# An attention kernel's context and output products moved later by one slot, and a key copy moved ahead of the divisions

## The chip, the cores and the metric

The kernel runs on one NeuronCore of a Trainium2 chip. The metric is the device time of one execution in microseconds, as the median of several runs. The engines are named as in the profile: PE is TensorE's matmul, PEld its weight load, DVE is VectorE, ACT is ScalarE, POOL is GpSimd and SP the engine that issues the DMAs.

## The reference

The input is x, 4 x 1024 tokens of 512 features, all in fp32. The result is x plus an attention of the layer-normalized x plus a matmul of it in rounded 8-bit floats. Cut to what matters here:

```python
xn = layernorm(x)
q  = rope(rmsnorm(xn @ Wq + bq))            # 16 heads of 128
lk = rope(rmsnorm(xn @ Wlk + blk)); lv = xn @ Wlv + blv
entries = weighted sums of each 4 tokens of xn        # 256 for each batch
ck = rope(rmsnorm(entries @ Wk + bk)); cv = entries @ Wv + bv
sparse = softmax(top 8 of causal(q @ ck.T)) @ cv
local  = softmax(band(q @ lk.T)) @ lv                 # this and the previous 128 tokens
out    = x + ((sparse + local) * 0.5) @ Wo + bo + fp8(xn) @ fp8(input2)
```

## The kernel before

The tokens are cut into 32 tiles of 128 (8 for each batch of 1024; the tile's number in its batch is called c). The 16 heads make 8 units of two heads. So there are 256 pairs of a tile and a unit, numbered n = 8t + u, and the main loop runs over slots s, each of which works on several of them at different stages. The order of the instructions on every engine is the order of the program (a manual schedule); each engine works its own list in that order, and only data and buffers hold it up.

The steps of a unit n, with the slot in which each stands before the change:

- `queries(n)` in slot n-3: q and local keys of two heads in one PSUM bank `qp`, eight matmul rows of 512 columns (L591).
- `squares`, `spread` (slot n-3, ACT and POOL) and `normalize`, `go_on_rotating`, `end_rotation` (slot n-2, DVE and POOL): the norms and the rotation.
- `turn_keys` and `fetch_keys` (slot n-2): DVE transposes blocks, SP stores them to DRAM and fetches them turned, as `qT` and `lkT`. In the first tile TensorE turns them instead.
- `values_of(n)` in slot n-1: the value projection, eight matmul rows of 256 columns (L697); `keep_values` copies it to `lv`.
- `scores(n, h)` at the head of slot n: for each head, against the previous tile's keys, this tile's keys and the entries' keys `ckT` (L739, L746, L749), into two PSUM banks `sc`. There is one such buffer.
- `weigh`, `settle`, `divide` in slot n: mask, top 8, exponentials (L799, L807), sums, and the division of the probabilities on ACT (L832).
- `turn(n)` in slot n: DVE transposes the probabilities in blocks of 32 to `probB` (L850), and SP stores them to DRAM (L858, `pr`). `fetch(n)` at the end of slot n: SP fetches them turned as `probT` in four DMAs (L892). `probT` has one buffer.
- `values(n)` in slot n+1: the context, up to 16 matmul rows of 128 columns (L909), with `probT` as the moving operand.
- `keep_context(n)` in slot n+2: ACT copies the context to `cT` (L924).
- `to_output(n)` in slot n+2: the product with Wo (L942), four matmul rows of 512 columns, accumulated over the eight units of a tile in one PSUM bank `out`, of which there is one. Behind unit 7, DVE adds the bank to the tile `x_sum` (L951), and SP stores the tile.

In a steady slot TensorE's order is scores(s), queries(s+3), to_output(s-2), values_of(s+1), values(s-1). `by_dma(n)` is true for the units from 8 to 252, whose probabilities are turned by DMA; for the others TensorE turns them (`turn_here`, `keep_turned`).

Beside this, generators are advanced at fixed places of a slot by `steps()` and `until(...)`. `chunk_prep` normalizes a later tile and pools its tokens to entries; in tiles 1 to 3 it runs for two tiles at once. `chunk_entries` makes the keys and values of new entries: it begins at u = 4 of a tile in `made` (0 to 4, then every fourth from 7 to 27), and its last step, at u = 7, turns the keys on TensorE (L557) and copies them to `ckT` on ACT (L558). `chunk_eight` makes the 8-bit product of a tile (L573). All of them and `values_of` share two PSUM banks `pp`.

The last three units stand behind the loop, written out by hand.

Of the kernel before, what the change touches and what calls it, by code (L numbers as in the profile page):

```python
# [38 lines left out]
def kernel(  # L39
# [30 lines left out]
    NCH = S // P  # L70
    NU = NH // 2
# [421 lines left out]
    def chunk_entries(g, n):  # L493

        b, half = divmod(g, NCH // GC)
        if b not in entries:
            entries[b] = (
                work.tile([P, 2 * P], F32, tag="ckT", name=f"ckT_{b}"),
                [None, None],
            )  # L500
        ckT, cv = entries[b]
        if n == 1:
            few = few_here[0]
        else:
            few = work.tile([P, HID], F32, tag="kv", name=f"fewT_{g}_{n}", bufs=1)
            if n < GC:
                nc.gpsimd.memset(few, 0.0)
            if not g:
                nc.sync.dma_start(few[:, 0 : NE * KK], few_here[1])
            turned = pooled[g].rearrange("c (a i) (b x) -> b i (c a) x", a=NB, b=NB)  # L510
            lo = 0 if g else 1
            for i in range(NB):
                nc.sync.dma_start(
                    few[ds(i * BLK, BLK), lo * P : n * P].rearrange("i (a x) -> i a x", x=BLK),
                    turned[i][:, lo * NB : n * NB],
                )
        few = few.rearrange("p (n k) -> p n k", k=KK)
        cse = cse_here if n == 1 else load_entry_angles(half)
        yield "A4"
        ep = pp(f"ep_{g}_{n}")  # L520
        for k in range(KK):
            nc.tensor.matmul(  # L522
                ep[:, 0 : 2 * D],
                few[:, :, k],
                wkv_sb[:, k, :],
                start=(k == 0),
                stop=(k == KK - 1),
            )
        yield "A5"
        kv = work.tile([P, HID], F32, tag="kv", name=f"kv_{g}_{n}", bufs=1)  # L530
        spare = kv[:, 2 * D :]
        kv = kv[:, 0 : 2 * D].rearrange("p (h d) -> p h d", h=2)
        nc.vector.tensor_tensor(
            kv.rearrange("p h d -> p (h d)"), ep[:, 0 : 2 * D], bkv_sb, ALU.add
        )

        cv[half] = work.tile([P, D], F32, tag=f"cv_{half}", name=f"cv_{g}_{n}")
        nc.scalar.copy(cv[half], kv[:, 1, :])
        ess = work.tile([P, 1], F32, tag="ess", name=f"ess_{g}_{n}", bufs=1)
        square_sum(ess, kv[:, 0, :], f"e{g}_{n}")  # L540
        er = rstd_of(ess, 1, 1.0 / D, EPS_RMS, f"er_{g}_{n}")
        yield "B5"
        ck = kv[:, 0:1, :]
        nc.vector.scalar_tensor_tensor(
            ck[:, 0, :], ck[:, 0, :], er, norm_w[:, 1, :], ALU.mult, ALU.mult
        )
        rotation = rotate(
            ck, cse, 1, spare[:, 0:ROPE], f"e{g}_{n}", spare[:, ROPE : 2 * ROPE]
        )
        next(rotation)  # L550
        next(rotation)
        yield "A6"
        for _ in rotation:
            pass
        yield "B6"
        cp = pp(f"cp_{g}_{n}")
        nc.tensor.transpose(cp[:, 0:P], ck[:, 0, :], ident)  # L557
        nc.scalar.copy(ckT[:, ts(half, P)], cp[:, 0:P])  # L558
        yield "A7"

# [79 lines left out]
    def by_dma(n):  # L640

        return NU <= n < NN - 3
# [292 lines left out]
    def to_output(n):  # L935
        t, u = place(n)
        b, c = divmod(t, NCH)
        if u == 0:
            outs[t] = psum.tile([P, HID], F32, tag="out", name=f"op_{t}", bufs=1)
        op, cT = outs[t], units[n].pop("cT")  # L940
        for h in range(2):
            nc.tensor.matmul(  # L942
                op,
                cT[:, h, :],
                wo_sb[u][:, h, :],
                start=(u == 0 and h == 0),
                stop=(u == NU - 1 and h == 1),
            )
        if u == NU - 1:
            xt = x_tiles.pop(("sum", t))  # L950
            nc.vector.tensor_tensor(xt, xt, op, ALU.add)  # L951
            nc.sync.dma_start(out[b, ts(c, P), :], xt)
# [15 lines left out]
    def for_unit(n, *todo):  # L968
        if 0 <= n < NN:
            for f, *more in todo:  # L970
                f(n, *more)
# [29 lines left out]
    for s in range(-3, NN - 3):  # L1001
        t, u = place(s)

        if u == 6 and t + 1 in ready:
            regular = chunk_prep(ready[t + 1][0])
        if u == 3 and 0 <= t < NT:
            load_x(t, "sum")
        if u == 4 and t in made:
            begun = chunk_entries(*made[t])
            next(begun)  # L1010
        if u == 5 and t in made:
            running.append(begun)
        if u == 5 and 0 <= t < NT:
            running.append(chunk_eight(t))
        if u == 4 and 0 <= t and t + 1 in ready:
            load_x(ready[t + 1][0], "norm")

        for_unit(s, (scores, 0), (scores, 1))
        for_unit(s - 2, (keep_context,))
        if s < NU - 1:  # L1020
            for_unit(s + 1, (turn_keys_here,), (keep_keys,))
        for_unit(s, (weigh,))
        for_unit(s + 3, (queries,))
        if s < 0:
            if s == -3:
                for _ in first:
                    pass
            if s == -1:
                until(start, "A7")
        for_unit(s + 2, (normalize,))  # L1030
        for_unit(s, (settle,))
        for_unit(s, (divide,))

        if 0 <= s < NU:
            fold_first_row(s)
        for_unit(s + 2, (go_on_rotating,), (end_rotation,))
        if by_dma(s):
            turn(s)
        if s + 2 >= NU:
            for_unit(s + 2, (turn_keys,))  # L1040
        steps()
        host = t if u < 4 else t + 1
        if host in ready:
            until(regular, FIRST_HALF.get(u))
        two = len(ready.get(t, ())) == 2
        if two and u == 2:
            extra = chunk_prep(ready[t][1])
        if two:
            until(extra, FIRST_HALF_MORE.get(u))
        for_unit(s + 3, (squares, (0, 1, 2, 3)), (spread,))  # L1050
        for_unit(s - 2, (to_output,))
        steps()
        if host in ready:
            until(regular, SECOND_HALF.get(u))
        if two:
            until(extra, SECOND_HALF_MORE.get(u))
        for_unit(s + 1, (values_of,))
        if not by_dma(s):
            for_unit(s, (turn_here,))
        for_unit(s - 1, (values,))  # L1060
        if by_dma(s):
            fetch(s)
        else:
            for_unit(s, (keep_turned,))
        if s + 2 >= NU:
            for_unit(s + 2, (fetch_keys,))
        for to, what in stores:
            nc.sync.dma_start(to, what)
        stores.clear()
        if u == 2 and 0 <= t < NT - 1:  # L1070
            fetch_tokens(t + 1)
        if u == 3 and 0 <= t < NT - 1:
            fetch_with_ones(t + 1)
        if two and u == 1:
            load_x(ready[t][1], "norm", True)
        for_unit(s + 1, (keep_values,))
        if s == -2:
            until(start, "B5")
        if s < NU:

            if s == -2:
                late_loads()
            if s == -1:
                late_constants()
                for k in range(KK):
                    nc.sync.dma_start(w2_raw[k], input2[ts(k, P), :])
            if 0 <= s < KK:
                for _ in range(4):
                    next(rounding, None)
            if 3 <= s + 6 < NU:  # L1090
                load_wqk(s + 6, nc.sync)
            if 3 <= s + 4 < NU:
                load_wlv(s + 4, nc.sync)
            if 0 <= s + 1 < NU:
                load_wo(s + 1, nc.sync)
        if u == 6 and 0 <= t and t + 2 < NT:
            load_angles(t + 2)
        units.pop(s - 1 - NU, None)


    a, b, c = range(NN - 3, NN)
    eight = chunk_eight(NT - 1)
    next(eight)
    for_unit(a, (scores, 0), (scores, 1))
    keep_context(a - 2)
    weigh(a)
    normalize(c)
    settle(a)
    divide(a)
    go_on_rotating(c)  # L1110
    end_rotation(c)
    turn_keys(c)
    to_output(a - 2)
    for n in (b, c):
        values_of(n)
        keep_values(n)
    fetch_keys(c)
    for_unit(b, (scores, 0), (scores, 1))
    next(eight)
# [20 lines left out]
    for _ in eight:  # L1140
        pass
    to_output(b)
    for_unit(c, (turn_here,), (keep_turned,), (values,), (keep_context,), (to_output,))


# [44 lines left out]
```

## Time and profile before

| what | us |
|---|---|
| median of 3 runs | 2650.33 (2649.67 to 2651.03) |
| the profiled execution's own time | 2650.34 |
| its span, from the first to the last instruction | 2648.6 |
| PE busy | 2608.5 (98%) |
| PEld busy | 1785.3 (67%) |
| DVE busy | 2215.5 (84%) |
| ACT busy | 1391.1 (53%) |
| POOL busy | 781.6 (30%) |

The granted TensorE clock is 0.999 of full speed over the span. The ends of matmuls are modelled and the matmuls overlap, so durations of a PE row are not to be added; the starts are. A row of a group has the busy time, the mean of one instruction in ns, and the engine's idle time before it with what ended it. A row of the waits has the total, the number and the longest.

### The profile page before, as it was taken

The numbers are of one execution on the slowest core, as the hardware profiler recorded it, in microseconds if no ns is written. First come the engines' busy times: TensorE is split into PE (matmuls) and PEld (weight loads), VectorE is DVE, ScalarE is ACT, GpSimd is POOL, SyncE is SP. The second block draws the span as 40 slices with busy tenths as digits, with TensorE's granted clock in tenths as the row PEclk, the third lists the DMA queues.
The fourth block names the chain that finished last, engine by engine and source line by source line (L and its number), as shares of the span: only waits on it lengthen the run. The fifth ranks groups of instructions, "written<-read, shape, count | busy, mean of one in ns | idle before, by whom it ended". The sixth has DMA issues, their size and how long they took to land.

```text
span 2648.6 us, 46831 instructions
## 1 busy us (share of the span) xinstructions
PE 2608.5 (98%) x11852; PEld 1785.3 (67%) x11887; DVE 2215.5 (84%) x8381; ACT 1391.1 (53%) x5560; POOL 781.6 (30%) x1128
## 2 busy tenths in 40 slices
PE   7999999999999999999999999999999999999998
PEld 4666667677666666766766666667676666676776
DVE  6878888888888888888988888888888888877886
ACT  3545545555555555555555555555555555554555
POOL 3422333223332223232233222232323332322222
PEclk9999999999999999999999999999999999999999
DMA  7355556665655555666655556665665555566554
GB/s 252 100 151 159 146 143 177 177 167 160 165 143 158 158 149 162 165 175 174 163 154 145 157 150 159 170 167 160 173 178 146 149 148 150 150 168 172 158 151 112
DMA packets 721004, 421.15 MB, mean 159 GB/s; under 512 B 395599, under 2 KB 670304, under 8 KB 720736
## 3 DMA queue, kind: packets, MB, share of 16 engines
q1 hardware_dynamic: 720128, 417.75, 58.2%
q8 instruction: 97, 1.59, 0.3%
q14 instruction: 171, 1.40, 0.2%
q10 hardware_dynamic: 608, 0.41, 0.1%
HBM read 224.75 MB, written 193.20 MB: 158 GB/s over the span
## 4 chain that ended last, share of the span: by engine, by line
PE 84%; DVE 7%; ACT 3%; DMA 2%; SPq 1%; issue 1%; POOL 1%; ACTq 0%; DVEq 0%; POOLq 0%
PE qp L591 28%; PE op L942 14%; PE vp L697 14%; PE cp L909 13%; PE sc L749 5%; PE sc L746 4%; PE sc L739 4%; ACT prob L832 1%; ACT prob L799 1%; PE fp L573 1%; DVE sc L771 1%; DVE taken L797 1%; DVE probB L850 1%; SPq L680 1%; PE ep L522 1%
## 5 line engine op out<-in xcount | busy, mean ns | idle before, releaser
L591 PE MATMUL qp<-wqk,xnT 128*128 128x512 f32 x1552 | 709.4, 593 | 4.8 <-DMA wqk<-in_L_attn_Wlk_dram 4.8
L799 ACT ACTIVATE prob<-sc,neg 128x256 f32<-128x256 f32 (+1 forms) x512 | 236.1, 461 | 773.6 <-DVE taken L797 752.4
L591 PEld LDWEIGHTS qp<-wqk,xnT 128*128 128x128 f32 x1552 | 294.9, 190 | 373.3 <-issue 370.9
L832 ACT ACTIVATE prob<-prob,tot 128x256 f32<-128x256 f32 (+7 forms) x1024 | 381.9, 443 | 296.7 <-DVE tot L825 296.7
L697 PEld LDWEIGHTS vp<-wlv,xnT 128*128 128x128 f32 x2048 | 389.0, 190 | 161.6 <-issue 115.3
L697 PE MATMUL vp<-wlv,xnT 128*128 128x256 f32 x2048 | 483.7, 379 | 0.1
L942 PE MATMUL op<-wo,cT 128*128 128x512 f32 x1024 | 481.6, 593 | 1.6 <-ACT cT L924 1.5
L323 POOL TENSOR_TENSOR rb<-th,cs 128x256 f32<-128x256 f32 x256 | 204.0, 797 | 743.8 <-DVE th L619 740.0
L771 DVE CUSTOM_DVE_ANT_0 sc<-sc,mask_b 128x256 f32<-128x256 f32 (+1 forms) x512 | 211.9, 414 | 182.6 <-PE sc L749 172.1
L942 PEld LDWEIGHTS op<-wo,cT 128*128 128x128 f32 x1024 | 193.6, 190 | 227.3 <-issue 185.3
L850 DVE STREAM_TRANSPOSE probB<-prob 128x512 f32<-128x512 f32 (+2 forms) x490 | 306.0, 629 | 10.9 <-ACT prob L832 0.2
L301 POOL TENSOR_SCALAR r<-ss 128x4 f32<-128x4 f32 x256 | 57.7, 226 | 846.8 <-ACT junk L307 844.1
L909 PE MATMUL cp<-probT,lv 128*128 128x128 f32 x1920 | 298.6, 275 | 5.8 <-DMA probT<-pr 4.4
L307 ACT ACTIVATE junk<-qp 128x128 bf16<-128x128 f32 x1024 | 278.6, 272 | 30.0 <-PE qp L599 5.6
L909 PEld LDWEIGHTS cp<-probT,lv 128*128 128x128 f32 x1920 | 273.3, 191 | 23.2 <-issue 10.1
L619 DVE SCALAR_TENSOR_TENSOR th<-qp,r,norm_w 128x128 f32<-128x128 f32 x1024 | 286.2, 342 | 1.9 <-POOL r L302 1.5
L302 POOL TENSOR_TENSOR r<-r,nhalf 128x4 f32<-128x4 f32 x256 | 265.1, 1035 | 21.4
L815 DVE SCALAR_TENSOR_TENSOR prob<-taken,prob 128x128 f32<-128x128 bf16 (+7 forms) x512 | 186.4, 365 | 97.6 <-ACT prob L807 96.4
L591 PE MATMUL qp<-wqk,xone 128*128 128x512 f32 x496 | 258.3, 602 | 1.6 <-DMA xone<-xb_dram 1.4
L909 PE MATMUL cp<-probT,cv 128*128 128x128 f32 x1536 | 255.2, 275 | 0.0
L749 PE MATMUL sc<-ckT,qT 128*128 128x96 f32 (+7 forms) x1024 | 226.7, 303 | 7.0 <-ACT ckT L558 7.0
L909 PEld LDWEIGHTS cp<-probT,cv 128*128 128x128 f32 x1536 | 212.7, 192 | 0.0
(141 smaller groups left out, 3670.5 us busy)
## 6 DMA issues: line engine op xcount, KB each, us to landing
pr<-probB SPq DMA_DIRECT2D x125, 512.0 KB
probT<-pr SPq DMA_DIRECT2D x500, 128.0 KB
qk<-thb SPq DMA_DIRECT2D x992, 64.0 KB
pr<-probB SPq DMA_DIRECT2D x96, 384.0 KB
probT<-pr SPq DMA_DIRECT2D x384, 96.0 KB
qT<-qk SPq DMA_DIRECT2D x248, 128.0 KB
lkT<-qk SPq DMA_DIRECT2D x248, 128.0 KB
x_norm<-_attn_hidden_states_dram SPq DMA_DIRECT2D x32, 256.0 KB
```

Of the source, the lines that this page charges most:

```text
L302: nc.gpsimd.tensor_tensor(r, r, nhalf[: ss.shape[0], 0:n], ALU.pow)
L307: nc.scalar.activation(junk[: src.shape[0]], src, AF.Square, accum_out=acc)
L591: nc.tensor.matmul(qp, xnT[:, k, :] if k or not t else xone, wqk_sb[u][:, k, :], start=(k == 0), stop=(t > 0 and k == KK - 1),)
L619: nc.vector.scalar_tensor_tensor(th[:, i, :], qp[:, ts(i, D)], r[:, i : i + 1], norm_w[:, i // 2, :], ALU.mult, ALU.mult,)
L697: nc.tensor.matmul(vp[:, 0:256], xnT[:, k, :], wlv_sb[u][:, k, :], start=(k == 0), stop=(k == KK - 1),)
L749: nc.tensor.matmul(sc[:, spa], q, ckT[:, 0:m], start=True, stop=True)
L771: nc.vector.tensor_tensor_reduce(sc[h][:, loc], sc[h][:, loc], mask_b[:, loc], -1.0, TAKEN, ALU.add, ALU.min, neg[h][0],)
L799: nc.scalar.activation(probs[h][:, loc], sc[h][:, loc], AF.Exp, bias=neg[h][0], scale=-1.0, accum_out=tot[:, h, 0:1],)
L832: nc.scalar.mul(probs[h][:, cols], probs[h][:, cols], tot[:, h, part : part + 1])
L850: nc.vector.transpose(pb[:, :, ds(h * g, g), :], prob[:, parts[0] * P : (parts[-1] + 1) * P].rearrange("p (g b i) -> p b g i", b=NB, i=BLK),)
L909: nc.tensor.matmul(blocks(cp[:, h, :]), v, probT[:, :, h * len(parts) + i - parts[0], :], start=(i == parts[0]), stop=(i == parts[-1]),)
L942: nc.tensor.matmul(op, cT[:, h, :], wo_sb[u][:, h, :], start=(u == 0 and h == 0), stop=(u == NU - 1 and h == 1),)
```

## The change

The context product of a unit is made in slot n+2 instead of n+1, behind the queries. The fetch of the turned probabilities goes from the end of slot n into slot n+1, behind that product. The copy to `cT` follows the divisions of slot n+2. The product with Wo comes in slot n+3, directly behind the scores. The value projection of a unit from 8 on is made in its own slot instead of the one before. The addition that empties the output bank is split off as `end_output` and stays late in the slot in which the product of unit 7 is made. At u = 7 of a tile in `made`, the entries' keys are turned on TensorE directly behind the queries and copied to `ckT` ahead of the divisions. So a steady slot has on TensorE: scores(s), to_output(s-3), queries(s+3), values(s-2), values_of(s). The written-out end takes over what the loop now leaves undone.

```diff
         cp = pp(f"cp_{g}_{n}")
         nc.tensor.transpose(cp[:, 0:P], ck[:, 0, :], ident)
+        yield "turned"
         nc.scalar.copy(ckT[:, ts(half, P)], cp[:, 0:P])
         yield "A7"
...
+
+    def end_output(n):
+        t, u = place(n)
+        b, c = divmod(t, NCH)
+        op = outs[t]
         if u == NU - 1:
+            outs.pop(t)
             xt = x_tiles.pop(("sum", t))
             nc.vector.tensor_tensor(xt, xt, op, ALU.add)
             nc.sync.dma_start(out[b, ts(c, P), :], xt)
...
         for_unit(s, (scores, 0), (scores, 1))
-        for_unit(s - 2, (keep_context,))
+        if by_dma(s - 3):
+            to_output(s - 3)
+        if not by_dma(s - 2):
+            for_unit(s - 2, (keep_context,))
         if s < NU - 1:
             for_unit(s + 1, (turn_keys_here,), (keep_keys,))
         for_unit(s, (weigh,))
         for_unit(s + 3, (queries,))
+        if u == 7 and t in made:
+            running.remove(begun)
+            until(begun, "turned")
+
+        if by_dma(s - 2):
+            values(s - 2)
+        if by_dma(s - 1):
+            fetch(s - 1)
...
         for_unit(s + 2, (normalize,))
         for_unit(s, (settle,))
+        if u == 7 and t in made:
+            until(begun, "A7")
         for_unit(s, (divide,))
+        if by_dma(s - 2):
+            keep_context(s - 2)
...
         for_unit(s + 3, (squares, (0, 1, 2, 3)), (spread,))
-        for_unit(s - 2, (to_output,))
+        if s >= NU:
+            values_of(s)
+        if not by_dma(s - 2):
+            for_unit(s - 2, (to_output,), (end_output,))
+        if by_dma(s - 3):
+            end_output(s - 3)
...
-        for_unit(s + 1, (values_of,))
+        if s + 1 < NU:
+            for_unit(s + 1, (values_of,))
         if not by_dma(s):
             for_unit(s, (turn_here,))
-        for_unit(s - 1, (values,))
-        if by_dma(s):
-            fetch(s)
-        else:
+        if not by_dma(s - 1):
+            for_unit(s - 1, (values,))
+        if not by_dma(s):
             for_unit(s, (keep_turned,))
...
-        for_unit(s + 1, (keep_values,))
+        for_unit(s if s >= NU else s + 1 if s + 1 < NU else -1, (keep_values,))
...
     for_unit(a, (scores, 0), (scores, 1))
-    keep_context(a - 2)
+    to_output(a - 3)
     weigh(a)
+    values(a - 2)
+    fetch(a - 1)
     normalize(c)
     settle(a)
+    keep_context(a - 2)
     divide(a)
...
-    to_output(a - 2)
-    for n in (b, c):
+    for n in (a, b, c):
         values_of(n)
         keep_values(n)
+    to_output(a - 2)
     fetch_keys(c)
```

More of the change, by code (lines that the diff above doesn't have):

```diff
@@ L1097 @@
             load_angles(t + 2)
-        units.pop(s - 1 - NU, None)
+        units.pop(s - 3 - NU, None)
     a, b, c = range(NN - 3, NN)
@@ L1142 @@
     to_output(b)
-    for_unit(c, (turn_here,), (keep_turned,), (values,), (keep_context,), (to_output,))
+    for_unit(c, (turn_here,), (keep_turned,), (values,), (keep_context,), (to_output,), (end_output,))
 _INS = [
```

## The prediction

> **What bounds the kernel now.** I read the page first, then the waits by engine, then the timeline of one slot in the steady state, of the stretch from 150 to 380 us and of the end, and last the order of the two programs engine by engine. A slot is one turn of the main loop, with number s; u = s mod 8 is the unit within a tile of 128 tokens, and tile t = s div 8.
>
> ```profile
> PE 2608.5 (98%) x11852; PEld 1785.3 (67%) x11887; DVE 2215.5 (84%) x8381; ACT 1391.1 (53%) x5560; POOL 781.6 (30%) x1128
> PE 84%; DVE 7%; ACT 3%; DMA 2%; SPq 1%; issue 1%; POOL 1%; ACTq 0%; DVEq 0%; POOLq 0%
> L942 PE MATMUL op<-wo,cT 128*128 128x512 f32 x1024 | 481.6, 593 | 1.6 <-ACT cT L924 1.5
> ```
>
> TensorE is the bound. The mean of 593 ns is not what one matmul costs, since they overlap: from start to start the timeline has 429 ns at 512 columns, 216 at 256 and 110 to 118 at 128. So I count start-to-start steps and call a wait what a step has beyond these. The Trainium skill (Perfetto Trace Analysis, Identifying the Most-Contended Engine) says matmul busy time is a bad measure of headroom and weight-load busy a good one. By that row, 67%, a third of the span would be open to a better order. By the steps, slot 123 (1304.35 to 1314.82) has no wait at all: 1.82 scores, 3.43 queries, 1.72 output product, 1.73 value projection, 1.78 context product make its 10.47. All waits of the trace together come to about 40 us. I take the steps: the change issues the same matmuls and can only gain or lose in waits.
>
> ```profile
> PE sc L749 <- ACT ckT L558: 7.0, 6, 1.7
> PE qp L591 <- DMA wqk<-in_L_attn_Wlk_dram: 4.8, 1, 4.8
> PE cp L909 <- DMA probT<-pr: 4.4, 5, 1.6
> PE cp L557 <- DVE kv L328: 3.7, 3, 2.3
> PE op L942 <- ACT cT L924: 1.5, 3, 0.6
> DVE sc L771 <- PE sc L749: 172.1, 172, 2.6
> DVE qm_x L274 <- DMA pooled<-xb: 9.4, 3, 3.6
> DVE xb L364 <- DMA pooled<-xb: 8.3, 3, 2.9
> ```
>
> The targets are rows one, three and five: some 13 us (16 by steps, since each restart costs a little more). The last two rows matter as much: three tiles, t = 1 to 3, prepare two chunks each, and there VectorE stands still 2.8 us at u = 3 and 3.5 at u = 5 for a DMA. It falls 3.6 to 4.5 us behind the scores. There VectorE sets the pace, not TensorE.
>
> By place, TensorE's waits are: before slot 8, unchanged; slots 8 to 32, 15.5 us; slots 33 to 252, 5.7 us; the written-out end, 3.7 us.
>
> ```profile
> 1309.59 1.88 PE L942 MATMUL op<-wo,cT 128*128 128x512 f32 x4
> 1312.50 1.71 ACT L832 ACTIVATE prob<-prob,tot 128x256 f32<-128x256 f32 x4 [1.02 <-DVE tot L825]
> 1313.04 0.61 PE L909 MATMUL cp<-probT,lv 128*128 128x128 f32 x4
> 1315.81 0.64 ACT L924 ACTIVATE cT<-cp,blvT 128x128 f32<-128x128 f32 x2
> 1316.64 1.02 PE L591 MATMUL qp<-wqk,xone 128*128 128x512 f32 x2
> 1317.71 1.75 SPq L892 DMA_DIRECT2D probT<-pr  x4
> ```
>
> Here the context of unit s-1 closes slot 123, its copy to cT follows at 1315.81 behind the squares, and the product with Wo comes 3.8 us later. The fetch of probT goes out at 1317.71 and is needed at 1323.5: 5.8 us.
>
> **The change part by part.**
>
> *New order on TensorE.* Scores, output product of s-3, queries, (entries' turn), context product of s-2, value projection of s. No matmul is added. The neighbours' steps are the same (110 to 118 after a narrow one, full width after a wide one), so the order itself costs 0.
>
> *Fetch of probT.* It now stands ahead of the store of unit s on SP and waits for the context product of s-2, 8.8 us into the slot (1.82+1.72+3.43+1.78). Its four issues take 1.75: done at 10.6. Behind it stands the store of probB, ready when VectorE has transposed, 10.6 into slot 123 (1314.95): delay about 0 (up to 1.1 with fewer entries, where the store's reader has a slot to spare). What follows (keys' stores, their fetch) no longer stands behind a fetch. The data are needed 6.9 us after the issues. The DMA waits of slots 33 to 252 (0.61+0.77+0.58+0.33 on probT, 0.52 on xone) go.
>
> *Output product directly behind the scores.* Its cT is copied behind the divisions of unit s-1. In slot 123 these end at 1314.21; the next activation starts 0.1 before such an end and its first half is out 0.36 later (the first product waited 0.40 for a copy at 2642.43), so cT is ready at about 1314.5 and wanted at 1316.64. Cover: 2.1 us, on the row 1312.50. The smallest cover between t = 4 and the end is 1.1 us at u = 7 of late tiles, and none at three tile ends (below).
>
> What is moved with it on ScalarE: the copy to cT (0.64 us) now precedes the four squares instead of following them. The squares end 0.64 later, and r, for the next slot's normalization, with them: in slot 123 r is done at 1317.0, then at 1317.7, and it is read at 1320.03. Free. The value projection of unit s instead of s+1 leaves its copy lv two slots before its reader. The store of a finished tile moves one slot down on SP; nobody waits for it.
>
> *Keys ahead of the divisions.* At u = 7 the copy (0.25 us) falls in ScalarE's 1.02 us of idleness before L832: 0. The three waits of 0.92 at the batch ends (715, 1360, 2003 us) were for a copy behind the divisions. Now the output product waits there for cT behind the same divisions: wanted at 715.2, ready at 715.11+0.31: 0.25 each.
>
> *The output bank.* It is single. The add that frees it moves from slot u = 1 to u = 2 (0.68 us), and the next tile's first product comes 5.2 us later in PE's order before, but now only the scores after it. VectorE's end of slot u = 2, plus 0.68 and 0.05, against the start wanted: between 0.9 early and 0.16 late for t >= 4. About 1.0 us in all with VectorE's shifted lag. No row has this wait; its bounds are 0 and 28 x 0.65 = 18 us (a whole add exposed each time). I take 1.0, from the timelines.
>
> *Slots 8 to 32.* The deeper pipeline takes matmuls out of slot 7 (a value projection, 1.73), slot 9 (a context product, 1.34) and slot 10 (an output product, 1.72): 4.8 us. TensorE is then 5.0 us earlier at slot 11, but VectorE, whose own work leaves it 0.1 to 1.2 us per slot there, only 2.7. From slot 12 VectorE paces, and the product is held by the divisions. Slot 21: scores would end at 251.3 (before: 255.2, 3.9 earlier); the softmax of unit 20 starts at 246.6 (before: 249.52), its divisions end 6.5 later, cT at 253.4: wait 2.1. With slots 23 (2.6), 24 (0.9) and the bank at 19 (0.3), t = 2 has 5.9; by the same rule t = 1 has 6.1 and t = 3 has 5.8: 17.8 in place of 15.5 (4.3, 5.5, 5.7). The waits on ckT, probT, xone and kv turn into waits on cT.
>
> Can so long a wait drop the clock? After the gap of 5.0 us at 11.49 three matmuls took 0.85 us instead of 0.43, 1.4 us lost; after 2.46 us at 29.15 none. The Trainium skill (TensorE: Matmul & The Clock Gate, What's actually happening) halves the clock after an idle window of about 3.4 us. My longest waits are 2.95 and 2.62. By the rule 0; by the rows, which leave 2.46 to 5.01 open, up to 2 x 1.4 = 2.8. I take 0.
>
> *The end.* The 5 us of matmul come back here.
>
> ```profile
> 2620.41 0.47 PE L739 MATMUL sc<-lkT,qT 128*128 128x128 f32 x2 [1.00 <-DVE tot L825]
> 2629.53 0.50 PE L739 MATMUL sc<-lkT,qT 128*128 128x128 f32 x2 [0.91 <-DMA qT<-qk]
> ```
>
> These two waits (1.16 and 1.07 by steps) are filled by it. A new one: the third value projection needs a bank that ScalarE frees only behind the divisions of the first unit, 10.2 into the end where TensorE arrives at 8.8: 1.46. The other 1.5 stay: 2.9 for 3.7.
>
> *Sum.* (17.8-15.5) + (1.75-5.7) + (2.9-3.7) = -2.4 us. The profiled execution took 2650.34 (span 2648.6 and 1.7 around it), 0.01 from the median 2650.33. So 2647.9. A difference under 0.2% (5.3 us) can't be told from none here.
>
> **The rivals.**
>
> *No difference, as summed (0.50):* 2645.0 to 2655.6.
>
> *Faster (0.28): the early tiles lose their waits.* If VectorE's DMA stalls of 2.8 and 3.5 shrink because SP is less crowded behind the keys' stores, its lag shrinks and with it half of my 17.8: 2647.9-8.9 = 2639. For it: two of SP's key stores took 2.25 and 1.55 us there instead of 0.45, just ahead of the stores that VectorE waits for. Against: those stores keep their place directly behind the keys', and nothing is removed ahead of them.
>
> *Slower (0.22): the single output bank.* My margins of the add are 0.4 us on average. If the add lands 0.7 later than I set it, 25 of 28 tiles wait, some 10 us in all: 2658. It decides from about 0.65 late (8 us). For it: at u = 2 VectorE has no idle time in the 256-entry tiles. Against: in most tiles it then waits for scores.
>
> *It doesn't do what it says:* the order of the two programs shows that the moves are made.
>
> **How the numbers follow.** The point is the likeliest case. The range 2640 to 2659 leaves out about a tenth on either side: most of the faster rival beyond its middle, and a bank or clock cost of over 11 us.
>
> **What would show it.** Right: no PE wait on probT or ckT after 400 us; a new row of op on ACT cT of some 17 us, nearly all before 380; op on DVE under 2; SP's fetch waiting for PE cp. Wrong: op waits in every slot, or a PE wait on x_sum's add at each u = 3; PEclk below 9 near 170 or 280.

## The result, and the profile after

The changed kernel took 2657.98 us in the median (2653.56 to 2663.27) beside 2650.36 of the kernel before (2648.62 to 2651.03): ratio 1.0031, 95% interval 1.0023 to 1.0040. (A ratio and its interval come from all runs of both kernels, so it differs a little from the quotient of the medians.) It is slower, by little but beyond its interval. The profiled execution took 2656.96 us with a span of 2655.2, which is 6.6 us over the span before.

The page of the changed kernel first: busy shares, the shares of the chain that ended last, and the group of the product with Wo.

```profile
PE 2614.3 (98%) x11852; PEld 1789.6 (67%) x11887; DVE 2208.6 (83%) x8381; ACT 1382.1 (52%) x5560; POOL 776.0 (29%) x1128
PE 84%; DVE 7%; ACT 3%; DMA 3%; SPq 1%; issue 1%; POOL 0%; DVEq 0%; ACTq 0%
L943 PE MATMUL op<-wo,cT 128*128 128x512 f32 x1024 | 489.5, 601 | 9.1 <-ACT cT L925 7.2
```

Same instructions, same bound. PE's busy time rose by 5.8 us without one matmul more; a part of that, matmuls at a lower clock, comes back below. The waits of the changed kernel that matter here (engine, what waits, for what: total us, times, longest):

```profile
PE op L943 <- ACT cT L925: 7.2, 11, 0.9
PE sc L740 <- ACT prob L808: 6.1, 6, 2.4
PE sc L747 <- DMA lkT<-qk: 3.1, 3, 1.4
PE cp L910 <- DMA probT<-pr: 1.9, 3, 1.4
PE op L943 <- DVE x_sum L958: 1.5, 3, 0.5
PE vp L698 <- ACT lv L710: 1.2, 1, 1.2
PE sc L747 <- DVE qm_x L274: 1.2, 1, 1.2
DVE sc L772 <- PE sc L750: 163.8, 160, 3.6
DVE xb L364 <- DMA pooled<-xb: 11.9, 3, 4.6
DVE qm_x L274 <- DMA pooled<-xb: 11.2, 3, 4.1
```

The row on ckT is gone, as the change meant it. The row on probT is not, and a new one stands above it: scores that wait for lkT, the local keys, which no PE row of before names. (By its place, the scores of u = 6 of tile 24, the row on qm_x is one more of these; what a row names behind the arrow is inferred.) VectorE's two stalls on pooled grew by 5.4 us.

By place, as the difference of the starts of the slots (after minus before, negative is earlier), with three of the experiments beside it:

| kernel | up to slot 7 | 7 to 33 | 33 to 253 | 253 to the end | span |
|---|---|---|---|---|---|
| predicted | 0 | -2.5 | -4.0 | +4.0 | -2.4 |
| changed | -1.1 | -0.8 | +4.3 | +4.2 | +6.6 |
| pr stored behind the keys | +2.8 | +0.4 | -4.5 | +4.2 | +2.9 |
| product behind the queries | +2.5 | -4.5 | +1.4 | +4.2 | +3.6 |
| both, end repaired | +2.4 | -3.3 | -5.3 | +2.7 | -3.5 |

The change does nothing in the first column. It holds the arrival of the first weights (slot 0 starts at 30.30 us in the changed kernel and at 31.31 before) and the granted clock, 0.97 over the first 110 us in the changed kernel, 0.98 before and 0.94 with pr stored behind the keys; both differ from one execution to the next. So the columns behind it are compared, more than the span. The end came as predicted. The middle, slots 33 to 253, missed by 8.3 us: that is the question.

Its waits, as excess over the start-to-start steps, are lkT 1.60, 1.46 and 1.32 at u = 6 of tiles 8, 16 and 24, and 0.51, 0.29 and 0.17 elsewhere; probT 1.53, 0.47 and 0.34; together 7.7 us where the prediction had none. Who held lkT back is read from SP's waits. Before:

```profile
SPq L858 <- DVE probB L850: 755.0, 223, 6.8
SPq L690 <- DMA qk<-thb: 7.0, 13, 2.1
```

After:

```profile
SPq L691 <- DMA qk<-thb: 394.5, 318, 3.3
SPq L893 <- PE cp L910: 322.8, 159, 4.0
```

Before, SP waited mostly for VectorE. Now it waits, slot after slot, for the keys' own stores to land, before it can fetch them (L691): 394.5 us for 7.0. The fetch of probT used to stand between those stores and that fetch, and its four issues covered the landing. The change took it out, put it ahead of the stores, and gave it a wait for TensorE. SP's timeline shows both (start, length, then what is issued), for the keys of unit 70. Before:

```profile
759.72 0.38 SPq L858 DMA_DIRECT2D pr<-probB  x1
760.19 1.89 SPq L680 DMA_DIRECT2D qk<-thb  x4
762.79 1.73 SPq L892 DMA_DIRECT2D probT<-pr  x4
764.71 0.38 SPq L690 DMA_DIRECT2D qT<-qk  x1
765.13 0.51 SPq L690 DMA_DIRECT2D lkT<-qk  x1
```

After:

```profile
758.41 0.41 SPq L105 DMA_DIRECT2D x_norm<-_attn_hidden_states_dram  x1
758.93 3.10 SPq L893 DMA_DIRECT2D probT<-pr  x4
762.15 0.36 SPq L859 DMA_DIRECT2D pr<-probB  x1
762.62 1.94 SPq L681 DMA_DIRECT2D qk<-thb  x4
766.03 0.38 SPq L691 DMA_DIRECT2D qT<-qk  x1
766.46 0.51 SPq L691 DMA_DIRECT2D lkT<-qk  x1
```

Slot 69 began at 760.50 before and at 759.08 after. So the keys' stores went out 0.3 us ahead of the slot before, and 3.5 into it after. SP then stands still from 764.56 to 766.03, and lkT leaves 7.4 us into the slot instead of 4.6. The scores of slot 70 wait, by the timeline of TensorE:

```profile
769.46 0.47 PE L747 MATMUL sc<-lkT,qT 128*128 128x128 f32 x2 [1.44 <-DMA lkT<-qk]
```

A slot of the first tile of a batch lasts 8.71 us. SP needs some 6.9 there now (1.9 fetch, 0.4 store, 1.9 stores, 1.4 idle, 0.9 fetch, and the gaps), and 2.8 more where pooled, xone and x_norm are loaded, as at u = 3 and 4: more than a slot. What is late adds up until u = 6. At tile 24 the stores also took longer to land: SP stood still there for 3.1 us.

### The profile page after: what moved, and what is told of

The parts are those of the page before. It is cut to its first block, busy times and chain, and to the rows that moved or that the text cites. A ratio compares the mean times of both kernels' runs of the same rounds, so it can differ in the third digit from the quotient of the medians.

```text
span 2655.2 us, 46696 instructions
## 1 busy us (share of the span) xinstructions
PE 2614.3 (98%) x11852; PEld 1789.6 (67%) x11887; DVE 2208.6 (83%) x8381; ACT 1382.1 (52%) x5560; POOL 776.0 (29%) x1128
## 3 DMA queue, kind: packets, MB, share of 16 engines
q14 instruction: 170, 1.39, 0.2%
## 4 chain that ended last, share of the span: by engine, by line
PE 84%; DVE 7%; ACT 3%; DMA 3%; SPq 1%; issue 1%; POOL 0%; DVEq 0%; ACTq 0%
PE qp L592 28%; PE op L943 15%; PE vp L698 14%; PE cp L910 13%; PE sc L750 5%; PE sc L747 4%; PE sc L740 3%; ACT prob L833 1%; ACT prob L800 1%; PE fp L574 1%; DVE sc L772 1%; SPq L681 1%; DVE taken L798 1%; PE ep L522 1%; DMA qk<-thb 1%
## 5 line engine op out<-in xcount | busy, mean ns | idle before, releaser
L943 PE MATMUL op<-wo,cT 128*128 128x512 f32 x1024 | 489.5, 601 | 9.1 <-ACT cT L925 7.2
L698 PEld LDWEIGHTS vp<-wlv,xnT 128*128 128x128 f32 x2048 | 373.6, 190 | 49.8 <-issue 2.6
L943 PEld LDWEIGHTS op<-wo,cT 128*128 128x128 f32 x1024 | 182.5, 191 | 140.6 <-issue 109.6
```

Of the source, the lines that this page charges most:

```text
L698: nc.tensor.matmul(vp[:, 0:256], xnT[:, k, :], wlv_sb[u][:, k, :], start=(k == 0), stop=(k == KK - 1),)
L943: nc.tensor.matmul(op, cT[:, h, :], wo_sb[u][:, h, :], start=(u == 0 and h == 0), stop=(u == NU - 1 and h == 1),)
```

## The experiments

The kernel before ran beside each group, with medians of 2649.36 (the first four), 2648.57 (the next four) and 2649.75 us (the last four). So ratios to before are compared.

**1. The fetch behind the keys' stores again.**

```diff
-        if by_dma(s - 1):
-            fetch(s - 1)
...
+        if by_dma(s - 1):
+            fetch(s - 1)
         if s + 2 >= NU:
             for_unit(s + 2, (fetch_keys,))
```

> The changed kernel with one place altered: the fetch of probT for unit s-1 stands on SP where the fetch stood before the change, behind the store of the probabilities and the stores of the keys, directly ahead of the fetch of the keys. Theory 1 (SP's order: the fetch in mid-slot, with its wait for the context product, pushes the stores of the keys back, so that lkT comes late): the PE waits on lkT of 1.60, 1.46 and 1.32 us at u = 6 of the tiles 8, 16 and 24 and the three smaller ones go, 5.3 us in all; the waits on probT (2.3 us) stay within 1 to 4, because the fetch goes out no earlier than before the change and is wanted 1.6 us earlier in the slot; sum 2651 to 2654. Theory 2 (it is the traffic: the DMA engines are slower because transfers now bunch): the lkT waits at u = 6 stay above 1 us each, and the time stays at 2656 to 2659.

2725.28 us, ratio 1.0279 (1.0264 to 1.0293). No expectation came near. The waits of its TensorE:

```profile
PE cp L910 <- DMA probT<-pr: 61.6, 64, 3.8
```

No PE row names lkT, as theory 1 has it. But the fetch went out at 1306.78, 2.4 us into the slot that began at 1304.36, and the context product, 7.1 into it at 1311.46, still waited 0.14: from first issue to landing some 4.7 us, all the time there was. Before, the same place left it 5.8 us. So the new order, which asks for probT 1.6 us earlier in the slot, needs the early fetch; its price is SP's idleness.

**2. The keys' copy alone**, put into the kernel before.

```diff
+        if u == 7 and t in made:
+            running.remove(begun)
+            until(begun, "turned")
...
         for_unit(s, (settle,))
+        if u == 7 and t in made:
+            until(begun, "A7")
         for_unit(s, (divide,))
```

> The kernel before with only the last part of the change: at u = 7 the entries' keys are turned directly behind the queries and copied to ckT ahead of the divisions. Theory 1 (the copy was late only because it stood behind the divisions): the three waits of the scores on ckT of 0.92 us go and the 1.74 us at tile 3 shrinks; 2.7 to 4.5 us less than before, 2646 to 2647.6. Theory 2 (the softmax of that slot holds the next scores anyway, since there is one buffer of scores, or the turn comes too early for the entries' keys and TensorE waits for VectorE's kv): the waits come back on other names, and the time is within 1 us of before.

2645.08 us, ratio 0.9978 (0.9968 to 0.9987); in the last group 2644.09, 0.9983 (0.9975 to 0.9990). The size of theory 1, though not its place: slots 7 to 33 gained 4.5 us; the three batch ends kept 0.4 to 0.7 of their 0.92 each, since other waits moved in (at 722.19 the context product waited 0.53 for probT). This part of the change is good by itself, so the moves beside it cost more than the 0.3% by which the whole is slower: some 0.5%, from 0.9978 to 1.0031.

**3. The product behind the queries.**

```diff
-        if by_dma(s - 3):
-            to_output(s - 3)
...
+        if by_dma(s - 3):
+            to_output(s - 3)
         if by_dma(s - 2):
             values(s - 2)
```

> The changed kernel with the product of unit s-3 with Wo put behind the queries of its slot instead of directly behind the scores, which gives cT and the output bank 3.4 us more. Theory 1 (VectorE sets the pace in the tiles 1 to 3, and the product only shows it): the ten or so waits of op on cT of about 1 us between 160 and 380 us leave their row and come back as waits of the scores on prob or of the context product; what is really gained is the 1.2 us of cT at the batch ends, the 1.5 us of the output bank and at most 3 us of the early tiles: 2651 to 2655. Theory 2 (each of these waits is a cost of its own, and they take the TensorE clock down with them near 168 and 280 us): 9 us of waits and 2.6 us of halved clock go, 2643 to 2646.

2652.98 us, ratio 1.0013 (1.0006 to 1.0019), the time of theory 1. Waits of its TensorE:

```profile
PE sc L740 <- ACT prob L808: 7.8, 6, 2.4
PE sc L747 <- DMA lkT<-qk: 3.3, 4, 1.9
PE cp L910 <- DMA probT<-pr: 2.7, 3, 1.4
```

Of the rows of op, that on x_sum is gone and that on cT is down to 0.5, at the very end. In the early tiles most came back under other names. The rows of op had 6.9 us between 160 and 390 us; here the scores wait 1.7 more for the softmax (7.8 for 6.1), the turn of the entries' keys 1.6 for VectorE, and 2.0 are new on lkT and probT. From start to start, slots 7 to 33 took 3.7 us less than in the changed kernel, where theory 1 had at most 3 for them, and slots 33 to 253 took 2.9 less, about what cT and the bank cost there. The late DMAs of the middle are untouched.

**4. The new order from unit 32 on only**, so that the 4.8 us of matmul leave slots in which TensorE sets the pace.

```diff
+    def late(n):
+        return 4 * NU <= n < NN - 3
...
-        if by_dma(s - 3):
+        if late(s - 3):
             to_output(s - 3)
...
-        if s >= NU:
+        if s >= 4 * NU:
             values_of(s)
```

> The changed kernel with the new order only from unit 32 on; the units 8 to 31 keep the order of before (the keys' copy ahead of the divisions stays in all tiles). Theory 1 (the 4.8 us of matmul that the longer pipeline takes out of its first three slots are lost in the change, because VectorE sets the pace there, and are paid at the end all the same): here they leave the slots 31 to 34, where TensorE sets the pace, and are gained in full: the early tiles cost what they cost before (15.5 us of waits), slot 35 starts 4 to 5 us earlier than before, and the sum is 2 to 4 us below the changed kernel, 2653 to 2656. Theory 2 (the early tiles gained what they could under the new order, 1.3 us net): the time is 1 us above the changed kernel or more, 2658 to 2661.

2656.06 us, ratio 1.0024 (1.0016 to 1.0031). The mechanism of theory 1 shows: from slot 31 to 35 its start went from 1.55 to 6.03 us ahead of before, 4.5 gained. At slot 40 it was 1.71 ahead: lkT 0.24 and 0.75, cT 0.77, prob 0.36 and probT 1.77 had eaten it. The sum can hardly be told from the changed kernel.

**5. Other work in SP's gap: the loads.**

```diff
-        if s + 2 >= NU:
-            for_unit(s + 2, (fetch_keys,))
         for to, what in stores:
             nc.sync.dma_start(to, what)
...
+        if s + 2 >= NU:
+            for_unit(s + 2, (fetch_keys,))
```

> The changed kernel with the loads of a later tile (tokens turned at u = 2, their row of ones at u = 3, and the stores of rounded tokens) issued ahead of the fetch of the keys instead of behind it; the fetch of probT keeps its early place. Theory 1 (SP is overfull: since the change it stands idle at the fetch of the keys until their stores have landed, 394.5 us in all where it was 7.0, and with the loads on top a short slot of 8.71 us is not enough; loads in that gap are free): SP's wait at the fetch of the keys falls by 1 us or more in each of those slots, the PE waits on lkT of 1.3 to 1.6 us at u = 6 of tiles 8, 16 and 24 shrink to under 0.5 each, 3 to 4 us in all, 2653 to 2655. Theory 2 (the landing is slow because of the traffic, not the queue): the fetch of the keys now comes behind the loads and lkT is as late or later; 2657 to 2661.

2654.59 us, ratio 1.0023 (1.0014 to 1.0033). SP's wait for the landing fell from 394.5 us:

```profile
SPq L691 <- DMA qk<-thb: 247.6, 210, 3.3
```

From slot 33 on three waits on lkT are left, 0.17, 0.17 and 0.37, and slots 33 to 253 take 3.2 us less than before where the changed kernel took 4.3 more. So theory 2 (traffic) does not explain the middle: the same bytes move here, in another order. But slots 7 to 33 became 1.8 us longer than in the changed kernel.

**6. Other work in SP's gap: the store of pr.**

```diff
         if s + 2 >= NU:
             for_unit(s + 2, (turn_keys,))
+        if by_dma(s):
+            store_turned(s)      # the store of pr, taken out of turn(s)
```

> The changed kernel with the store of the probabilities (pr) issued on SP behind the four stores of the keys instead of ahead of them: it has a slot to spare now, and it fills part of the time in which SP waits for the keys to land. Theory 1 (SP is overfull in the short slots): some 0.45 us a slot come free, the lkT waits fall by about that much each and further where the delay adds up over two or three slots, probT stays at about 2 us; 2654 to 2656. Theory 2 (VectorE's single probB is what limits: a later store keeps it occupied and the next transposition waits): new waits of DVE on the store of pr, and no gain or a loss, 2657 to 2662.

2651.84 us, ratio 1.0009 (1.0001 to 1.0018): better than theory 1, which kept 2 us on probT, and no row of VectorE waits for the store of pr, as theory 2 had it. All rows of its TensorE's waits between 400 and 2600 us:

```profile
PE op L946 <- ACT cT L928: 0.7, 3, 0.2
PE op L946 <- DVE x_sum L961: 0.5, 1, 0.5
```

The same window of the changed kernel has 3.1 on lkT, 1.9 on probT and 1.2 on qm_x besides. SP's waits:

```profile
SPq L896 <- PE cp L913: 488.8, 200, 5.5
SPq L691 <- DMA qk<-thb: 200.2, 327, 2.4
```

The idle time at the keys' fetch was halved, and SP now arrives early at the fetch of probT and waits for TensorE there, which delays nothing that TensorE waits for. One store of 0.45 us on the other side of four others took away every DMA wait of the middle; with it the middle is what the prediction summed.

**7 and 8. Four repairs together** (5, 6, 3 and the end), in all tiles, and with experiment 4's `late` in place of `by_dma`. The end:

```diff
     keep_context(a - 2)
+    values_of(a)
+    keep_values(a)
     divide(a)
...
-    for n in (a, b, c):
+    for n in (b, c):
```

> The changed kernel with four things together: the loads ahead of the fetch of the keys, the keys' stores ahead of the store of pr, the product with Wo behind the queries, and in the written-out end the first of the three value projections with its copy ahead of the divisions. Theory 1 (each failed term of the sum has its own cause, and the repairs add): the product behind the queries takes 5 us off the changed kernel as it did alone, the loads 3, the store 1, the end 1.4: 2647 to 2650, about the time of before. Theory 2 (the DMA waits come from the depth of the pipeline itself, and a fetch saved in one place is late in another): 2651 to 2654, no better than the product behind the queries alone.

2654.18 us, ratio 1.0019 (1.0010 to 1.0027): just above theory 2's range. Waits on lkT came back (4.2 us).

> The same four repairs, with the new order only from unit 32 on, where the last such kernel gained 4.5 us over slots 31 to 35. Theory 1 (the longer pipeline is worth having if it is filled where TensorE sets the pace and SP is not overfull): 4.5 gained, 4.1 given back at the end, and the waits between slots 36 and 253 under 4 us: 2644 to 2647, as fast as the kernel of before with the keys' copy alone (2645.1) or faster. Theory 2 (what is gained at slot 31 is lost again within two tiles to late DMAs, as it was in the last such kernel): 2648 to 2653.

2671.89 us, ratio 1.0088 (1.0075 to 1.0101), far off both. It lost 21 us in slots 7 to 33: the scores waited 15.8 us for qT, where the order of before already has the fetch of probT in the gap; as I read it, the loads ahead then only make the keys later. No run took the two edits apart there.

**9 to 11. Without the loads ahead.** First experiment 4 with the end repaired and the store of pr behind the keys from unit 32 on:

```diff
-        if by_dma(s):
+        if late(s):
             store_turned(s)
```

> The changed kernel with the new order from unit 32 on only, from there the keys' stores ahead of the store of pr, and the end repaired (first value projection with its copy ahead of the divisions). Theory 1 (the late keys' fetch was the one thing that ate the gain, and the store moved behind cures it without costing the early tiles): 4.5 us gained over slots 31 to 35 and 4 us over slots 40 to 253 against before, 4.1 given back at the end: 2643 to 2646. Theory 2 (behind slot 35 TensorE is so far ahead that DMAs are late all the same): probT or lkT waits of 4 us or more come back, 2647 to 2651.

2646.18 us, ratio 0.9986 (0.9980 to 0.9993), between the two. By place, 4.97 us were gained from slot 33 to 253 and the end gave back 2.7 instead of 4.2; a probT wait of 1.69 at 432 stayed. Then with experiment 3's diff on top, for `late` units:

> As the kernel before it, and the product with Wo behind the queries, from unit 32 on. Theory 1 (the waits on cT at the batch ends, 0.41 us three times, and on the output bank, 1.5 us in all, are costs of their own): 2.5 us less than the kernel before it, 2641 to 2644, with no PE wait on ACT cT or DVE x_sum between 400 us and the end. Theory 2 (with the product there the DMAs of the short slots come late again, as in the kernel with all four repairs): lkT waits of 2 us or more in all, no gain, 2644 to 2648.

2642.02 us, ratio 0.9975 (0.9966 to 0.9984). Theory 1: between 440 and 2600 us TensorE waits for nothing at all. And experiments 3, 6 and the end together in all tiles:

> The changed kernel, new order in all tiles from unit 8 on, with the product behind the queries, the keys' stores ahead of the store of pr, and the end repaired, but without the loads ahead of the fetch of the keys. Theory 1 (in the kernel with all four repairs it was the loads ahead that made qT and the early tiles late): 4 to 6 us below that one, 2647 to 2650, the remainder against before being the early tiles, where VectorE takes the 4.8 us that the pipeline gives. Theory 2 (product and stores don't add): 2651 to 2655.

2643.84 us, ratio 0.9978 (0.9971 to 0.9984), better than expected. It differs from experiment 7 in the loads alone: these cost 0.4% there, where the store already fills the gap. By place, 6.5 us of that lie in slots 7 to 33, where the loads ahead had cost 1.8 by themselves, and 2.5 in slots 33 to 253. Two cures for one gap didn't add. The last run is experiment 2 again, told there:

> The kernel before with only the keys' copy ahead of the divisions, beside the repaired kernels on one chip, to tell which is the fastest. All theories: 0.2 to 0.3% below before, as it was, 2643 to 2646.

Experiments 2, 9, 10 and 11 beat both given kernels; their intervals overlap, so which of them is fastest stays open.

## Why the prediction was wrong

- **The step that failed: "Fetch of probT".** It held that the delay of the store behind it was "about 0" ("up to 1.1 with fewer entries") and that "what follows (keys' stores, their fetch) no longer stands behind a fetch", and so struck out all DMA waits of slots 33 to 252. The fetch did go ahead of the store of pr, but also of the keys' stores, and where it had stood it had covered their landing. I priced its delay only for the store of pr, whose reader has a slot to spare, and not for the keys, whose reader has none. And I priced it in slot 123, which lasts 10.47 us: there the store of pr went out 11.1 us into the slot for 10.6 before, but in slot 68, of 8.71 us, it went out 3.8 us later than before. Cost: 7.7 us where the sum had 0, of the 8.3 by which slots 33 to 253 missed. Experiments 5 and 6 show it: with work in the gap the waits from slot 33 on shrink to 0.7 or vanish, and slots 33 to 253 give -3.2 and -4.5 against the -4.0 of the sum.
- **The clock, taken at 0, cost about 2.6 us**, as bounded (2.8). Windows of the changed kernel (stretch and its length; busy time and number for PE, PEld, DVE, ACT and POOL):

```profile
160.00:172.00 12.00, 9.51 (x39) 6.54 (x38) 10.73 (x44) 5.17 (x22) 1.74 (x4) 0.86 0.50 110
276.00:283.00 7.00, 6.07 (x19) 3.12 (x19) 6.60 (x24) 3.56 (x15) 3.18 (x6) 0.76 0.32 101
283.00:290.00 7.00, 7.00 (x40) 5.45 (x39) 6.15 (x22) 4.64 (x17) 3.25 (x6) 1.00 0.39 98
```

  The last three numbers are the granted clock, the busy share of the DMA engines and GB/s. The first stretch follows a wait of 2.51 us at 165.24. In the second, starts of the product are 0.85 us apart instead of 0.43; it follows two waits of 0.92 and 1.10 within 2.6 us, and I had asked about the longest single wait. This is more than the 1.7 us that slots 7 to 33 missed (-0.8 for -2.5), and part of the 5.8 us of busy time.
- **Right, with sizes a little small:** the waits on cT at the batch ends were 0.39 to 0.40 for 0.25; the output bank 1.45 for 1.0. The rival of the bank is refuted: behind tile 3 four tiles wait for the add, not 25. The ckT row went. The end gave +4.2 for +4.0, its new wait on lv 1.39 for 1.46; experiments 7 to 11 take that wait out and return 1.5 us.
- **The early tiles:** I put all of their waits on cT (17.8); half stand on scores behind prob. That VectorE paces there is borne out in part by experiment 3: of the 6.9 us of op, 3.3 came back as waits for the softmax and VectorE and 2.0 as late DMAs, and slots 7 to 33 still became 3.7 us shorter. That the 4.8 us are lost there is borne out by experiment 4.
- **The faster rival had its sign wrong:** VectorE's stalls on pooled grew by 5.4 us. Those stores keep their place behind the keys' stores, and the keys' stores went later; whether that is the cause is not shown, since the stalls stay at 23.6 and 24.4 us in experiments 5 and 6 (23.1 in the changed kernel).
- **Luck:** the slower rival's 2658 is the time that was measured, but for a reason that was not among the rivals: a fetch moved on SP, not the bank.

## What to carry to other kernels

An instruction in an in-order queue is also a cover for what stands around it. Before moving a transfer, list what waits between its neighbours (here a store, and the fetch of what it stored); what it leaves behind loses its cover, and what it is put ahead of is late by its issues and by its own wait. Then budget that queue by slot, for the shortest slot with the most loads. And when one gap has been filled, a second cure for it can be a new delay.

## What was not expected of the hardware

The granted clock fell after shorter stops than the idle window of about 3.4 us that the Trainium skill names (TensorE: Matmul & The Clock Gate, What's actually happening). In the kernel of experiment 11 the scores waited 2.31 us at 253.89, and the queries behind them ran at half rate. A wait of 1.97 us at 341.16 in the same kernel was followed by no such steps, nor was the pair of 1.26 and 1.10 at 252 in the changed kernel. So no bound on one wait separates the cases.

The traces show in part what does. In all fourteen, the stretches at half clock begin and end on a fixed grid of 3.41 us, to within 0.02 us; the grid lies differently in each run. Cut along it, the kernel of experiment 11 has (columns as above):

```profile
251.53:254.94 3.41, 1.26 (x10) 1.05 (x9) 2.90 (x16) 1.70 (x7) 0.72 (x1) 1.00 0.34 71
254.94:258.36 3.42, 3.42 (x10) 1.87 (x9) 3.10 (x11) 1.76 (x7) 0.00 (x0) 0.50 0.59 107
336.86:340.27 3.41, 2.50 (x15) 1.94 (x14) 3.24 (x17) 0.70 (x3) 0.53 (x1) 1.00 0.46 79
340.27:343.68 3.41, 2.52 (x15) 2.04 (x16) 2.71 (x12) 2.54 (x10) 0.72 (x1) 1.00 0.36 65
```

The wait of 2.31 us fell whole into one step and left 1.26 us of PE in it; the next step ran at half clock. The wait of 1.97 was split by the edge at 340.27, which left 2.50 and 2.52. The changed kernel:

```profile
251.11:254.52 3.41, 1.96 (x13) 1.79 (x14) 2.78 (x12) 2.41 (x9) 0.72 (x1) 1.00 0.40 80
275.00:278.41 3.41, 1.90 (x13) 1.74 (x14) 2.78 (x12) 2.52 (x10) 0.72 (x1) 1.00 0.23 73
278.41:281.83 3.42, 3.42 (x5) 1.36 (x5) 3.31 (x12) 1.57 (x9) 2.18 (x4) 0.50 0.62 192
```

Over the fourteen traces, from 60 us on and counting steps at full clock: where PE was busy for less than 0.42 of a step, the next one ran at half clock each time (23 steps); above 0.56 it never did; in between it did in 5 of 21 steps. What decides in between stays open. So what a wait costs here hangs also on where the grid lies in that run.
